# Loading the first weights in halves and the first condition ahead of a threshold, in a conditioned ternary feed-forward kernel

## The chip, the cores and the metric

The kernel runs on one core of one Trainium2 chip. Its time is the device time of one execution in microseconds (us); a version is measured in several runs, and the median is compared. Five engines work side by side: TensorE (PE in the profile; its weight loads are PEld), VectorE (DVE), ScalarE (ACT), GpSimd (POOL) and SyncE (SP), which here issues nearly all transfers. Each takes its own instructions in program order and waits for the others through semaphores.

## The reference

x has 128 sequences of 64 channels and 512 positions. Each sequence picks one of 200 conditioning matrices, and a feed-forward layer with ternary weights follows; its result is quantized to 4 bits and added to x. Cut to what matters:

```python
w = weights[conditions]                       # (128, 64, 64), gathered
c = einsum('bct,bcd->bdt', x, w)              # the condition: (128, 64, 512)

def ternarize(W):                             # threshold 0.05
    delta = 0.05 * max(abs(W))                # over the whole matrix
    mask  = abs(W) > delta
    alpha = sum(abs(W) * mask) / max(sum(mask), 1)
    return alpha * sign(W) * mask

h = gelu(c @ ternarize(W1).T + b1)            # 512 -> 2048
y = h @ ternarize(W2).T + b2                  # 2048 -> 512
scale = max(abs(y)) / 7 + 1e-8                # over the whole of y
out = x + clip(round(y / scale), -7, 7) * scale
```

The threshold `delta` needs the largest magnitude of all of W1, so no ternary weight exists before the last piece of W1 has landed.

## The kernel before, in words

The 128 sequences go through in 16 blocks of 8 (four pairs, `PAIRS = 4`, 512 columns). The hidden layer of 2048 is cut into 16 chunks `hc` of 128. Per block and chunk, PE multiplies the condition by the chunk's W1 (`layer1`), ScalarE applies Gelu, and PE multiplies by the chunk's W2 (`layer2`). A value is carried as a high part (fp32r) and a low part (f16), so each product is made twice, `k = 0` and `k = 1`; for the high part GpSimd widens the ternary weights to fp32r (`widen1`, line 369).

The order of all work is written out by hand: every engine is wrapped in `InOrder` (line 28), which keeps its instructions in program order. Nothing is planned by a scheduler. A semaphore that a transfer uses is used again by the eighth transfer after it, which waits for it.

The change concerns the start, before the first block's chunks flow:

- *Loads* (lines 104 to 131). SyncE issues, in this order: `conditions` (the token numbers, 32 KB) into the tile `first`; the four groups of W1 (`nat1`, 1 MB each; how each is cut into pieces stands in `PIECES`, line 113: groups 0 and 1 whole, group 2 in two, group 3 in three); x of block 0 in two halves of two pairs (`load_x`, line 95); b1; W2; b2.
- *Rows and gathers.* DVE makes row numbers from the token numbers (`rows`, five small instructions), and GpSimd gathers one pair's matrices after the other from HBM (`fetch`, line 166; an indirect transfer of 128 rows of 256 bytes).
- *Group by group* (lines 282 to 295), DVE takes the largest magnitude of each piece (`top_1`), and ScalarE makes the signs (`sign1`) and the magnitudes (`abs1`, in place, so after DVE's reduction of the same piece).
- *Warm-up.* PE runs 46 matmuls with no use for their result (`idle`, line 276), issued ahead of all its other work.
- *`diag`.* GpSimd writes the gathered matrices into the diagonal blocks of `diag`, all four pairs in two instructions (`place_all`, line 183; `place`, line 178, does one pair in two).
- *Threshold* (`thresholds`, line 228). It is a generator: DVE reduces `top_1` to one column and spreads it to 128x128 in `first`, PE transposes that (`tops`), and after the first `yield` DVE takes the maximum and makes `delta` and `minus`.
- *Conditions of block 0.* `mix0(j)` (line 300) is pair j's condition on PE; `hi0(j)` copies its high part on ScalarE, `lo0(j)` makes its low part on DVE.
- *Ternary weights of W1.* `mask1` and `signed1` on DVE make a group's ternary weights, the first group in two halves (`parts1`), of two chunks each.
- *First chunks.* `early(hc)` (line 503) makes chunk hc of block 0 into a PSUM bank; chunk 0 in two halves of 256 columns, each of which needs only two pairs. `count1` counts the mask's ones on PE.

These lines set the order around the change; each name queues on its own engine:

```python
315  find = thresholds("w1", top_1, first[:, 3, :P])
316  next(find)                    # up to PE's transpose
317  delta1, minus1 = next(find)
318  for j in range(PAIRS):
319      mix0(j)
```

and from line 600 on: first half of `mask1(0)` and `signed1(0)`; two gathers of block 1; `widen1` of chunks 0 and 1; two more gathers; the rest of `lo0` and `hi0`; `early(0)`, `early(1)`; the second half of `mask1(0)` and `signed1(0)`; `widen1` of chunks 2 and 3; `count1(0)`; `early(2)`.

Of the kernel before, what the change touches and what calls it, by code (L numbers as in the profile page):

```python
# [15 lines left out]
AF = mybir.ActivationFunctionType  # L16
# [23 lines left out]
def tile_cond_ternary_ffn(  # L40
# [12 lines left out]
    pe, act, dve, pool, sp = (  # L53
        InOrder(tc, e) for e in (nc.tensor, nc.scalar, nc.vector, nc.gpsimd, nc.sync)
    )
    B, C, T = x.shape
# [4 lines left out]
    PAIRS = 4  # L61
    BLK = PAIRS * P
    NB = B // (2 * PAIRS)
    NG = 4
    GH = NH // NG
# [39 lines left out]
    first = big.tile([P, 4, P], F32, tag="big", name="first")  # L105
    cond_i, cond_f, wrap = (first[:, i, : B // 2] for i in range(3))
    cond_i = cond_i.bitcast(I32)
    sp.dma_start(out=cond_i, in_=conditions)


    nat1, nat2 = [], []

    PIECES = [[slice(0, GH)], [slice(0, GH)], [slice(0, 2), slice(2, GH)]]
    PIECES.append([slice(0, 2), slice(2, 3), slice(3, GH)])
    W1f = W1.rearrange("p k c h -> p k (c h)")
    for g in range(NG):
        w = big.tile([P, GH, T], F32, tag="big", name=f"nat1_{g}")
        for ks in PIECES[g]:
            sp.dma_start(out=w[:, ks, :], in_=W1f[:, g * GH :, :][:, ks, :])
# [36 lines left out]
    def half_of(h):  # L156
        return slice(h * C, (h + 1) * C)
# [20 lines left out]
    def place(n, j):  # L178
        for h in range(2):
            out = diag[half_of(h), j, h * D : (h + 1) * D]  # L180
            pool.tensor_scalar(out, gathered[n][half_of(h), j, :], UP, None, ALU.mult)

    def place_all(n):
        for h in range(2):
            out = diag[half_of(h), :, h * D : (h + 1) * D]
            pool.tensor_scalar(out, gathered[n][half_of(h)], UP, None, ALU.mult)
# [3 lines left out]
    def parts(n):  # L190
        return [
            big.tile([P, NT, BLK], t, tag="big", name=f"x{k}_{n}")
            for k, t in enumerate((F32R, F16))
        ]
# [6 lines left out]
    def pair_of(xt, j):  # L201
        return xt[j // 2][:, j % 2, :]

    def mix(xp, j, pc):

        for c in range(NT):
            pe.matmul(
                out=pc[:, c, :],
                lhsT=xp[:, c * P : (c + 1) * P],
                rhs=diag[:, j, :],  # L210
                start=True,
                stop=True,
            )
# [7 lines left out]
    def spread(top1, out, wide_top, space=ps_c, tag="pc"):  # L221

        dve.tensor_copy(wide_top, top1.to_broadcast([P, P]))
        tops = space.tile([P, P], F32, tag=tag, name=f"tops_{out.name}")
        pe.transpose(tops, wide_top, ident_f)
        return tops

    def thresholds(w, top, room):

        top1 = const.tile([P, 1], F32, name=f"top1_{w}")  # L230
        dve.tensor_reduce(top1, top, AX.X, ALU.max)
        delta = const.tile([P, 1], F32, name=f"delta_{w}")
        tops = spread(top1, delta, room)
        yield
        dve.tensor_reduce(delta, tops, AX.X, ALU.max)
        dve.tensor_scalar(delta, delta, THRESHOLD, None, ALU.mult)
        minus = const.tile([P, 1], F32, name=f"minus_{w}")
        dve.tensor_scalar(minus, delta, -1.0, None, ALU.mult)
        yield delta, minus
# [9 lines left out]
    def flat(w):  # L249
        return w.rearrange("p a b -> p (a b)")  # L250


    signs = [big.tile([P, 2, WCH], BF16, tag="big", name=f"signs_{i}") for i in range(2)]
# [3 lines left out]
    above = junk[:, 0, :]  # L257
    top_1 = const.tile([P, sum(map(len, PIECES))], F32)
    sums1 = const.tile([P, NG], F32)

    def group1(tiles, g):
        return tiles[g // 2][:, g % 2, :]

    def sign1(g):
        act.activation(group1(signs, g), flat(nat1[g]), AF.Sign)

    mags = nat1[: NG - 1]

    def abs1(g):

        if g == NG - 1:
            mags.append(big.tile([P, GH, T], F32, tag="big", name="mag"))
        act.activation(flat(mags[g]), flat(nat1[g]), AF.Abs)


    idle = ps_h.tile([P, T], F32, tag="ph", name="idle")
# [6 lines left out]
    for g in range(NG):  # L283
        for ks in PIECES[g]:
            dve.tensor_reduce(
                top_1[:, at : at + 1],
                flat(nat1[g][:, ks, :]),
                AX.X,
                ALU.max,
                apply_absolute_value=True,  # L290
            )
            at += 1
        if g < NG - 1:
            sign1(g)
            abs1(g)
    place_all(0)
    two_next = parts(0)
    pcs = []

    def mix0(j):  # L300
        home, tag = [(ps_c, "pc"), (ps_h, "ph"), (ps_y, "py0"), (ps_y, "py1")][j]
        pc = home.tile([P, NT, P], F32, tag=tag, name=f"pc_0_{j}")
        mix(pair_of(x_next, j), j, pc)
        pcs.append(pc)
# [4 lines left out]
    def lo0(j):  # L309
        part = slice(j * P, (j + 1) * P)  # L310
        dve.tensor_tensor(
            two_next[1][:, :, part], pcs[j], two_next[0][:, :, part], ALU.subtract
        )

    find = thresholds("w1", top_1, first[:, 3, :P])
    next(find)
    delta1, minus1 = next(find)
    for j in range(PAIRS):
        mix0(j)
    hi0(0)  # L320
    hi0(1)
# [1 line left out]
    def mask1(g, part=slice(0, WCH)):  # L323

        dve.tensor_scalar(
            group1(masks, g)[:, part], flat(mags[g])[:, part], delta1, None, ALU.is_gt
        )
# [64 lines left out]
    halves = slice(0, HALF), slice(HALF, BLK)  # L392
# [10 lines left out]
                    stop=(c == NT - 1 and k == 1),  # L403
                )

    def layer1_0(n, hc, ph, part=slice(0, BLK), between={}):
        g, i = divmod(hc, GH)
        narrow = group1(terns, g)[:, i * T : (i + 1) * T].rearrange("p (c h) -> p c h", c=NT)
        for k in range(2):
            w = narrow if k else wide1[n, hc]  # L410
            for c in range(NT):
                between.get((k, c), lambda: None)()
                pe.matmul(
                    out=ph,
                    lhsT=w[:, c, :],
                    rhs=cond[n][k][:, c, part],
                    start=(c == 0 and k == 0),
                    stop=(c == NT - 1 and k == 1),
                )
# [80 lines left out]
    ring = [t[:, i, :] for t in rings for i in range(2)]  # L500
    ring += [quarter.tile([P, BLK], F32, tag="quarter", name=f"ring_{i}") for i in (10, 11)]

    def early(hc, between={}):

        slot = (hc + 4) % 6
        if slot < 2:
            ph = ps_h.tile([P, BLK], F32, tag="ph", name=f"ph_0_{hc}")
        else:
            ph = ps_y.tile([P, BLK], F32, tag=f"py{slot - 2}", name=f"ph_0_{hc}")
        for part in halves if hc == 0 else [slice(0, BLK)]:  # L510
            layer1_0(0, hc, ph[:, part], part, between)
        waiting[hc] = ph

    def early_bend(hc):
        if hc % 2 == 0:
            pairs0[hc // 2] = big.tile([P, 2, 2, BLK], F32R, tag="big", name=f"h_{hc}")
        two = [pairs0[hc // 2][:, hc % 2, k, :] for k in range(2)]
        on_pool = hc in (0, 2, 4, 6)
        bend(0, hc, waiting.pop(hc), two, ring[hc % len(ring)], pool if on_pool else None)
# [91 lines left out]
    hi0(3)  # L611
    lo0(2)
    lo0(3)
    early(0)
    early(1)
    mask1(0, parts1[1])
    signed1(0, parts1[1])
    widen1(0, 2)
    widen1(0, 3)
    abs1(3)  # L620
    for g in range(NG):
        above1(g)
    number = ps_c.tile([P, 1], F32, tag="pc", name="number")
    count1(0)
    early(2)
    mask1(1)
    signed1(1)
# [24 lines left out]
    def behind(hc):  # L652
        if hc == 6:
            largest2(0)
        if 6 <= hc < 6 + NG - 1:
            largest2(hc - 5)
        if hc == 7:
            sign1(3)
        if hc == 8:
            signed1(3)  # L660
        if hc == 11:
            delta.extend(next(find))
            signed2(0)
        if hc == 12:
            for i in (1, 3):
                low(0, i)
            signed2(1)
        if hc in (13, 14):
            widen2(0, hc - 13)
# [19 lines left out]
    for hc in range(NH - LAG):  # L689
# [13 lines left out]
        if hc in (5, 7, 9, 11):  # L703
            j = (hc - 5) // 2
# [189 lines left out]
    order = [*range(AWAY, NB - 2), *range(AWAY), NB - 2]  # L894
# [211 lines left out]
    while s < len(steps):  # L1106
        n, hc = steps[s]
# [10 lines left out]
    n = NB - 1  # L1118
# [108 lines left out]
```

## Time and profile before

| | us |
|---|---|
| median of 3 runs (964.82 to 965.25) | 965.01 |
| the profiled execution's own time | 964.97 |
| its span, first to last instruction | 963.2 |
| PE busy | 951.2 (99%) |
| DVE busy | 708.2 (74%) |
| GpSimd busy | 703.7 (73%) |
| ScalarE busy | 637.1 (66%) |
| granted TensorE clock, mean | 0.999 |

The profile is one execution, and its times count from the start of the span. All compute instructions are recorded through the wrapper's line, L36, so groups are told apart by their tiles: `nat` is a weight matrix as loaded, `top` its largest magnitudes, `wg` the gathered matrices, `pc` a condition in PSUM, `x` its high and low parts, `terns` the ternary weights, `wf` the widened ones, `ph` a chunk in PSUM, `py` the second layer's result. A row of a timeline is start, length, engine, operation, output<-input and shapes, count, and in brackets the idle time before it with what ended it. The chain of waits follows the work that ended last back to the start. Idle time of an engine that nobody waits for costs nothing.

### The profile page before, as it was taken

The page shows a single profiled execution, that of the slowest core. Times are in us where ns is not written, and L with a number is a line of the kernel's source. Part 1 is how long each engine was busy: PE and PEld are TensorE (multiplying, and loading weights), DVE is VectorE, ACT ScalarE, POOL GpSimd, SP SyncE. Part 2 cuts the span into 40 slices and gives each one's busy share as a digit, 9 for nine tenths or more (in the row PEclk, how much of TensorE's full clock was granted, in tenths as well). Part 3 has the DMA queues.
Part 4 walks back from the last instruction along what each step waited for, and adds up shares of the span by engine and source line. Part 5 has one row for each costly group of instructions (what it writes and reads, how often), then busy time and mean ns, then how long its engine had stood idle before and what let it go on. Part 6 is the DMA issues. An engine that isn't in the chain of part 4 may idle for free.

```text
span 963.2 us, 17595 instructions
## 1 busy us (share of the span) xinstructions
PE 951.2 (99%) x6072; PEld 739.9 (77%) x6072; DVE 708.2 (74%) x1239; ACT 637.1 (66%) x1148; POOL 703.7 (73%) x1060
## 2 busy tenths in 40 slices
PE   8999999999999999999999999999999999999997
PEld 4687667888788787787778788788788878778774
DVE  7999766666676766666676676766667798888976
ACT  7995446656656566665656656666665777877774
POOL 5866867677686776767777686776767879788771
PEclk9999999999999999999999999999999999999999
DMA  9301011110111100111020111100131284575741
GB/s 357 103 23 47 14 33 49 33 60 15 35 49 34 60 24 28 55 36 49 25 69 15 34 50 33 59 26 24 49 128 53 65 289 168 191 239 183 274 180 67
DMA packets 33195, 80.11 MB, mean 83 GB/s; under 512 B 3792, under 2 KB 3792, under 8 KB 30160
## 3 DMA queue, kind: packets, MB, share of 16 engines
q1 hardware_dynamic: 31056, 76.86, 23.1%
q0 software_dynamic: 2048, 2.10, 0.7%
q8 instruction: 49, 0.80, 0.3%
q14 instruction: 42, 0.34, 0.1%
HBM read 46.44 MB, written 32.51 MB: 82 GB/s over the span
## 4 chain that ended last, share of the span: by engine, by line
PE 95%; DVE 2%; ACT 1%; DMA 1%; issue 0%; POOL 0%; SPq 0%; ACTq 0%; DVEq 0%
PE py L36 46%; PE xy L36 21%; PE z L36 16%; PE pc L36 6%; PE ph L36 6%; DMA nat<-in_L_ffn_W 1%; DVE top L36 1%; DVE xt L36 0%; ACT ring L36 0%; DVE y_last L36 0%; ACT diag L36 0%; DVE ring L36 0%; POOL wf L36 0%; ACT h L36 0%; PE number L36 0%
## 5 line engine op out<-in xcount | busy, mean ns | idle before, releaser
L36 PE MATMUL py<-wf,h 128*128 128x512 f32 x1088 | 316.2, 416 | 0.0
L36 POOL CAST wf<-w2t 128x512 fp32r<-128x512 fp8e4 x240 | 227.3, 966 | 106.7 <-PE py L36 103.6
L36 POOL CAST wf<-sums 128x256 fp32r<-128x256 fp8e4 (+1 forms) x336 | 181.2, 545 | 88.4 <-PE xy L36 85.0
L36 DVE SCALAR_TENSOR_TENSOR low_parts<-ring,h 128x512 f16<-128x512 f32 x232 | 206.0, 925 | 40.0 <-ACT h L36 40.0
L36 PEld LDWEIGHTS py<-wf,h 128*128 128x128 f32 x1088 | 196.5, 189 | 44.0
L36 ACT ACTIVATE ring<-ring,b1t,alpha_up 128x512 f32<-128x512 f32 x224 | 181.6, 818 | 63.4 <-DVE ring L36 58.6
L36 PE MATMUL py<-w2t,low_parts 128*128 128x512 fp8e4 x920 | 218.7, 379 | 0.0
L36 DVE TENSOR_TENSOR ring<-xy,ring 128x256 f32<-128x256 f32 x224 | 124.1, 554 | 120.3 <-PE xy L36 120.2
L36 ACT COPY ring<-xy 128x256 f32<-128x256 f32 x224 | 83.3, 372 | 174.0 <-PE xy L36 172.7
L36 PEld LDWEIGHTS <-low_parts 128*128 128x128 f16 x920 | 90.1, 98 | 84.1 <-issue 0.3
L36 ACT ACTIVATE h<-ring 128x512 fp32r<-128x512 f32 x240 | 138.6, 626 | 0.7
L36 POOL CAST wf<-w1t 128x256 fp32r<-128x256 fp8e4 (+1 forms) x240 | 132.5, 567 | 2.7 <-PE xy L36 0.3
L36 PE MATMUL xy<-xb,wf 128*128 128x256 f32 x448 | 98.8, 301 | 0.0
L36 PE MATMUL xy<-xt,wf 128*128 128x256 f32 x448 | 88.2, 278 | 1.0 <-ACT ring L36 0.6
L36 PE MATMUL xy<-xl,sums 128*128 128x256 f16 x448 | 87.9, 278 | 0.0
L36 PE MATMUL xy<-xl,w1t 128*128 128x256 f16 x448 | 86.6, 275 | 0.0
L36 PE MATMUL z<-xl,sums 128*128 128x256 f16 x448 | 85.5, 273 | 0.7 <-ACT ring L36 0.6
L36 PEld LDWEIGHTS xy<-xt,wf 128*128 128x128 f32 x448 | 76.2, 188 | 11.6 <-POOL wf L36 1.1
L36 PEld LDWEIGHTS xy<-xb,wf 128*128 128x128 f32 x448 | 75.8, 189 | 10.3
L36 PEld LDWEIGHTS <-sums 128*128 128x128 fp8e4 x896 | 69.2, 97 | 15.9 <-issue 1.2
L36 DVE TENSOR_TENSOR ring<-z,ring 128x256 f32<-128x256 f32 x112 | 47.2, 421 | 41.2 <-PE z L36 40.7
L36 POOL DMA_INDIRECT wg<-in_L_cond_weights,rows x64 | 64.0, 1000 | 18.3 <-issue 8.7
(126 smaller groups left out, 1342.2 us busy)
## 6 DMA issues: line engine op xcount, KB each, us to landing
xt<-in_x SPq DMA_DIRECT2D x36, 512.0 KB
y_dram<-y SPq DMA_DIRECT2D x15, 1024.0 KB
out<-xt SPq DMA_DIRECT2D x30, 512.0 KB
x_quarters<-in_x SPq DMA_DIRECT2D x56, 256.0 KB
nat<-in_L_ffn_W SPq DMA_DIRECT2D x6, 1024.0 KB
y_back<-y_dram SPq DMA_DIRECT2D x2, 1024.0 KB
nat<-in_L_ffn_W SPq DMA_DIRECT2D x3, 512.0 KB
wg<-in_L_cond_weights,rows POOLq DMA_INDIRECT x64, 2.5
```

The costliest lines, as they stand in the source:

```text
L36: return lambda *args, **kw: self._tc.keep_in_program_order(make(*args, **kw))
```

## The change

There are four edits, all at the start:

1. The token numbers are issued from ScalarE's queue; W1 is SyncE's first issue.
2. Group 0 of W1 is loaded in two halves, and its reductions, signs and magnitudes are made by halves.
3. `diag` is written pair by pair, and pair 0's condition stands ahead of the threshold's transpose on PE.
4. Chunks 0 and 1 are both made in halves of 256 columns, in a crosswise order (`early_two`): (chunk, half, k) = 000, 001, 010, 100, 101, 011, 110, 111.

```diff
-    sp.dma_start(out=cond_i, in_=conditions)
+    act.dma_start(out=cond_i, in_=conditions)
...
-    PIECES = [[slice(0, GH)], [slice(0, GH)], [slice(0, 2), slice(2, GH)]]
+    PIECES = [[slice(0, 2), slice(2, GH)], [slice(0, GH)], [slice(0, 2), slice(2, GH)]]
...
-    def sign1(g):
-        act.activation(group1(signs, g), flat(nat1[g]), AF.Sign)
+    def sign1(g, ks=slice(0, GH)):
+        out = group1(signs, g)[:, ks.start * T : ks.stop * T]
+        act.activation(out, flat(nat1[g][:, ks, :]), AF.Sign)
...
-    def abs1(g):
+    def abs1(g, ks=slice(0, GH)):
...
-        act.activation(flat(mags[g]), flat(nat1[g]), AF.Abs)
+        act.activation(flat(mags[g][:, ks, :]), flat(nat1[g][:, ks, :]), AF.Abs)
...
-            sign1(g)
-            abs1(g)
-    place_all(0)
+            pieces = PIECES[g] if g == 0 else [slice(0, GH)]
+            for ks in pieces:
+                sign1(g, ks)
+            for ks in pieces:
+                abs1(g, ks)
+    for j in range(PAIRS):
+        place(0, j)
...
     find = thresholds("w1", top_1, first[:, 3, :P])
+    mix0(0)
     next(find)
     delta1, minus1 = next(find)
-    for j in range(PAIRS):
+    for j in range(1, PAIRS):
         mix0(j)
...
-    def layer1_0(n, hc, ph, part=slice(0, BLK), between={}):
+    def layer1_0(n, hc, ph, part=slice(0, BLK), between={}, ks=range(2)):
...
-        for k in range(2):
+        for k in ks:
...
-    def early(hc, between={}):
+    def bank(hc):
...
-        for part in halves if hc == 0 else [slice(0, BLK)]:
-            layer1_0(0, hc, ph[:, part], part, between)
         waiting[hc] = ph
+        return ph
+
+    def early(hc, between={}):
+
+        layer1_0(0, hc, bank(hc), between=between)
+
+    def early_two():
+
+        phs = [bank(hc) for hc in range(2)]
+        order = [(0, 0, 0), (0, 0, 1), (0, 1, 0), (1, 0, 0), (1, 0, 1), (0, 1, 1)]
+        for hc, h, k in order + [(1, 1, 0), (1, 1, 1)]:
+            layer1_0(0, hc, phs[hc][:, halves[h]], halves[h], ks=(k,))
...
-    early(0)
-    early(1)
+    early_two()
```

## The prediction

> **What bounds the kernel now.** I read the page first: PE is busy 951.2 of 963.2 us, and the chain that ended last is 95% PE, so a change pays only where PE stands still. By stretches of time, PE lacks 3.8 us before 24.56 us (and 12.7 of its 20.8 busy ones there are warm-up matmuls), none from 24.56 to 62, 1.7 up to 950 and 6.5 in the last 13.2. The whole change acts in the first stretch. So I read next the chain of waits from the start, in order of time (start, length, what):
>
> ```profile
> 1.66 7.15 DMA nat<-in_L_ffn_W
> 8.84 6.86 DVE top L36 x6
> 16.20 0.33 PE tops_delta_w L36
> 16.53 3.60 PE pc L36 x32
> 20.14 0.59 ACT x L36
> 20.76 0.69 DVE x L36
> 21.45 0.67 DVE masks L36
> 22.15 0.70 DVE terns L36
> 22.91 1.61 POOL wf L36
> 24.56 3.90 PE ph L36 x16
> ```
>
> Seen here: W1's second group lands at 8.81; six reductions follow without a gap; then the threshold, the four conditions (`pc`), the last high and low part of x (`ACT x`, `DVE x`), the second half of group 0's mask and ternary weights, and GpSimd's widening for chunk 2. PE starts chunk 2 at 24.56 and has no gap for the next 37 us, so the end of the run moves with this moment. Then the timeline of single engines, with the idle time before each row:
>
> ```profile
> 1.19 3.64 SPq L36 DMA_DIRECT2D nat<-in_L_ffn_W  x7
> 2.66 0.29 DVE L36 CAST first<-first 128x64 f32<-128x64 int32 x1 [0.61 <-DMA first<-in_itok_B]
> 6.33 2.29 DVE L36 TENSOR_REDUCE top<-nat 128x1 f32<-128x2048 f32 x1 [2.37 <-DMA nat<-in_L_ffn_W]
> ...
> 4.25 1.17 POOL L36 DMA_INDIRECT wg<-in_L_cond_weights,rows  x1 [1.35 <-DVE rows L36]
> 14.07 1.78 POOL L36 TENSOR_SCALAR diag<-wg 64x256 f32<-64x256 f32 x2 [4.90 <-DMA wg<-in_L_cond_weights,rows]
> 16.12 1.01 POOL L36 DMA_INDIRECT wg<-in_L_cond_weights,rows  x1 [0.27 <-POOL diag L36]
> 17.43 1.29 POOL L36 DMA_INDIRECT wg<-in_L_cond_weights,rows  x1 [0.30 <-issue]
> 18.76 1.17 POOL L36 CAST wf<-terns 128x512 fp32r<-128x512 bf16 x2
> ...
> 20.76 0.69 DVE L36 TENSOR_TENSOR x<-pc,x 128x512 f16<-128x512 f32 x1 [0.20 <-ACT x L36]
> 22.91 6.25 POOL L36 CAST wf<-terns 128x512 fp32r<-128x512 bf16 x4 [0.60 <-DVE terns L36]
> 24.56 1.21 PE L36 MATMUL ph<-x,wf 128*128 128x512 f32 x4 [0.27 <-POOL wf L36]
> ```
>
> Three slacks stand here: DVE waits 0.20 us before the last low part, GpSimd 0.60 before the widening for chunk 2, PE 0.27 before chunk 2. GpSimd is a second chain as long as DVE's: token numbers land (2.66), `rows`, gathers, `diag`, two further gathers, and the first widening at 18.76 starts when the gather ahead of it ends at 18.72. Last, two tiles asked for by themselves: the gathers' time to landing, first in the first 40 us, then from 85 to 400 us, and the shapes that write `diag` (ns, minimum/median/maximum):
>
> ```profile
> DMA to landing us min/median/max: 5.4/5.8/6.4
> ...
> DMA to landing us min/median/max: 2.3/2.5/5.1
> ...
> L36 POOL TENSOR_SCALAR diag<-wg x116: 360/367/1812, 14.1 to 878.9; 64x64 f32<-64x64 f32 x112, 64x256 f32<-64x256 f32 x4
> ```
>
> **The change part by part.** Sums are against the profiled execution: 964.97 us, 963.2 of span and 1.77 around it; the median of the three runs is 965.01, so what is added to the one holds for the other within 0.04.
>
> *W1 first, in halves.* SyncE's first issue becomes W1's, so the stream starts 0.45 us earlier (1.19 against 0.74). Against that, group 0 now goes in two 512 KB pieces. SyncE's later issues, each of which waits for an earlier piece, come 1.43 us apart (10.26, 11.69, 13.12) for pieces of 512 KB, 2.86 per MB; the 1 MB piece of group 1 took 8.84 - 6.33 = 2.5. So halving costs 0 to 0.36, and group 1 lands 0.1 to 0.45 earlier; I take 0.25, the middle, since the gathers share the row with the 1.43. The halves themselves bring DVE nothing: group 0 is reduced before group 1 lands in either form. The six reductions then end at 15.44, and the threshold's input is ready at 15.9 instead of 16.15. ScalarE's Sign and Abs start earlier and end some 1.5 us earlier (18.1 to 16.6), so the first high part no longer waits for them; the later ones wait for PE. The extra reduction, two extra activations and the extra DMA issue lie in idle time of their engines (2.37 us before the first reduction, 4.10 before the first Sign, SyncE idle from 5.4); without that cover each costs under 0.5.
>
> *First condition ahead of the threshold.* PE takes its work in program order. Its warm-up matmuls end near 15.5. `mix0(0)` now comes next and waits for x's first half. That half follows W1's last piece (landed by 14.61, when the issue that waits for it goes out) by 512 KB, so about 1.4 us later, 16.0; the 0.25 makes it 15.75. One condition takes 3.60 / 4 = 0.90, so the threshold's transpose goes out at 16.65, not 16.20: 0.45 later, although its input is ready at 15.9. The bounds: +0.2 (x there before the warm-up ends: 15.5 + 0.9) and +0.7 (x as late as before). Behind it on DVE wait delta, the first mask, the first ternary half, and the four low parts. The last low part had 0.20 of slack; mask, ternary half and widening follow directly. So by DVE chunk 2 starts 0.45 - 0.20 = 0.25 later (0 to 0.5). The conditions end 0.45 earlier (0.90 moved forward, 0.45 lost), but that only feeds ScalarE's copies, which are then not late.
>
> *`place` pair by pair.* Two 64x256 instructions become eight of 64x64. In the build the first needs only the first gather, the other seven all four. Seven of 0.36 are 2.5 us against 1.78: GpSimd is 0.75 later (0.4 if they overlap as the two casts do, 1.17 for 2 x 0.61; 1.3 with the 0.44 from start to start that pairs of them show later). Behind them queue two gathers, the widenings for chunks 0 and 1, two more gathers, and the widening for chunk 2, whose slack is 0.60 plus DVE's 0.25. So this alone is covered; it uses up the cover.
>
> *Token numbers from ScalarE's queue.* This removes 0.45 from SyncE and adds a 0.39 us issue to ScalarE, which idles until W1 lands: nothing. But the 32 KB no longer go alone and first. They start together with the stream, on the same 16 DMA engines. Whatever later time (call it d) they land moves `rows`, the gathers, `diag` and all that GpSimd does up to chunk 2, one for one. The trace has no transfer on ScalarE's queue. Lower bound: 0, DVE takes them at 2.66 as now. Upper bound: a gather moves the same 128 rows of 256 bytes on a queue other than W1's, and needs 5.8 us to land under the stream, 2.5 without: 3.3. Between the two I take 1.0: the stream is only starting, and what competes is W1's first half, which I estimate to land at 6.33 - 0.45 - 1.25 + 0.1, about 4.7; even sharing to its end would be d = 2.0, and 1.0 is the middle of that and of no contention.
>
> The Trainium skill, DMA: Bandwidth & Descriptors, section Issuing engines are not separate DMA queues, says that DMAs from different engines interleave on the same 16 engines and that using several saves only issue time; its section Queues, rings and completion order has each DMA engine take turns packet by packet. By this rule the eight rows per engine would take turns with the eight of W1's half, d would be near 2.0 and the sum +2.2 us; the row of this case taken above gives +1.2.
>
> *Chunks 0 and 1 crosswise.* The 256-wide pieces take 0.56 and 0.37 us from start to start, the 512-wide 1.0 and 0.87, so the work is equal, 3.7 us. It fills PE's waits, but chunk 2 waits for GpSimd: from the first widening's end to chunk 2 PE needs 3.7 + 0.54 for the counts, GpSimd longer. Worth nothing while DVE or GpSimd is later; its cost is 0 to 0.1.
>
> **Sum.** Chunk 2 starts later by 0.25 + max(0, 0.75 + d - 0.85), at d = 1.0: 0.25 + 0.9 = 1.15 us. Behind it PE has next to no gap that could take it back. 964.97 + 1.15 gives 966.1.
>
> **The rivals.**
> - *Cancelled* (d under 0.3): the token numbers land as now, 0.1 to 0.5 us remain: 965.1 to 965.4. For it: ScalarE can issue at the same moment as SyncE. Against it: the gathers' 5.8 against 2.5.
> - *Slower by more than 0.2%* (1.93 us; about what a measurement of this kernel can tell from no change): one mechanism, the token numbers behind W1's halves. It decides from d = 1.8 on; at d = 2.0 the sum is 2.15, 967.1; at the full 3.3 it is 3.45, 968.4 (DVE's reductions would then also wait for `rows`). For it: the gathers' row, the even sharing. Against it: the engines are empty when both start.
> - *Faster*: the earlier stream reaches chunk 2. It needs x before 15.5, the threshold only 0.2 later, and d near 0; then DVE has 0.1 to give, and GpSimd's 0.60 bounds the rest: 964.4 to 964.9, not beyond 0.2%. Against it: `mix0(0)` stands before the threshold on PE in any case.
>
> **How the numbers follow.** Likeliest case (d from 0.3 to 1.8, 965.3 to 966.9): 0.48. Cancelled: 0.15. Slower beyond 0.2%: 0.31. Faster: 0.06, of which 0.03 beyond 0.2% by something that I don't see. So faster 0.03, same 0.66, slower 0.31. The range leaves out half of the faster cases and the top third of the slower: 964.8 to 967.9.
>
> **What will show it.** The first reduction near 4.7; group 1's near 8.6; the first gather's issue at 4.25 + d (this alone decides between the cases); the threshold's transpose at 16.65 right behind `mix0(0)`; the casts for chunk 2 starting near 24.1 with no wait for `terns`; PE's chunk 2 at 25.7, waiting for GpSimd. Wrong it would be if the token numbers land before 3, if PE shows gaps after chunk 2 that it didn't have, or if what lies around the span (1.77) grows with a second queue.

## The result and the profile after

The change makes the kernel slower by half a per cent. The changed kernel takes 970.37 us (median of six runs, 970.16 to 971.95) against 964.96 for the kernel before in the same sitting, 5.4 us more; the ratio on record, which is not the quotient of the two medians, is 1.0059, with a 95% interval from 1.0049 to 1.0069. The forecast of 966.1 and its range up to 967.9 are both missed. The profiled execution of the changed kernel took 970.16, its span is 968.4, so 1.76 lies around the span as before (1.77).

The moment to look at is again the start of chunk 2 on PE, 24.56 us before. This is the beginning of the chain of waits of the kernel after, in order of time (start, length, what):

```profile
0.74 4.34 DMA first<-in_itok_B
...
6.60 1.17 POOL wg L36
...
10.57 5.59 DMA wg<-in_L_cond_weights,rows
...
16.33 0.37 POOL diag L36
...
19.92 1.11 POOL wg L36
...
22.33 1.63 POOL wf L36 x2
...
24.11 1.71 POOL wg L36
...
26.12 0.91 POOL wg L36
...
28.28 0.63 POOL wf L36
...
28.95 3.88 PE ph L36 x16
```

Before, this stretch of the chain ran over W1, DVE's six reductions, PE's conditions and DVE's second mask. None of that is in it now. It is GpSimd's chain from end to end: token numbers, gathers, `diag`, two gathers, the first widenings, two gathers, the widening for chunk 2. (The row of 26.12 breaks off at a semaphore record inside the gather; the timeline has the gather whole, 2.15 us.) The timelines of the single engines in the same kernel give the times (start, length, engine, operation, and in brackets the idle time ahead of the row with what ended it):

```profile
4.92 1.06 ACT L36 ACTIVATE signs<-nat 128x1024 bf16<-128x1024 f32 x1 [2.25 <-DMA nat<-in_L_ffn_W]
...
5.10 0.20 DVE L36 CAST first<-first 128x64 f32<-128x64 int32 x1 [3.05 <-DMA first<-in_itok_B]
...
8.73 6.85 DVE L36 TENSOR_REDUCE top<-nat 128x1 f32<-128x2048 f32 x6 [0.17 <-DMA nat<-in_L_ffn_W]
...
18.06 0.29 DVE L36 TENSOR_REDUCE delta_w<-tops_delta_w 128x1 f32<-128x128 f32 x1 [2.02 <-PE tops_delta_w L36]
...
24.42 1.27 DVE L36 TENSOR_SCALAR masks<-nat,delta_w 128x2048 bf16<-128x2048 f32 x1
...
26.87 1.28 DVE L36 TENSOR_SCALAR masks<-nat,delta_w 128x2048 bf16<-128x2048 f32 x1
28.07 3.67 DVE L36 TENSOR_SCALAR masks<-mag,delta_w 128x2048 bf16<-128x2048 f32 x1
...
16.75 1.16 PE L36 MATMUL pc<-diag,xt 128*128 128x128 f32 x8 [1.42 <-POOL diag L36]
17.75 0.27 PE L36 MATMUL tops_delta_w<-ident_f,first 128*128 128x128 f32 x1
...
28.95 1.19 PE L36 MATMUL ph<-x,wf 128*128 128x512 f32 x4 [1.63 <-POOL wf L36]
...
16.33 3.31 POOL L36 TENSOR_SCALAR diag<-wg 64x64 f32<-64x64 f32 x7 [3.50 <-DMA wg<-in_L_cond_weights,rows]
...
24.11 1.71 POOL L36 DMA_INDIRECT wg<-in_L_cond_weights,rows  x1 [0.15 <-issue]
26.12 2.15 POOL L36 DMA_INDIRECT wg<-in_L_cond_weights,rows  x1 [0.30 <-issue]
28.28 2.27 POOL L36 CAST wf<-terns 128x512 fp32r<-128x512 bf16 x4
```

To be seen here: DVE takes the token numbers at 5.10, not at 2.66, and just 0.18 us after W1's first half became usable (ScalarE's first Sign, 4.92). DVE's reductions, 8.73 to 15.58, are as early as before, so the threshold's data are not the trouble. Yet the threshold's transpose goes out at 17.75 instead of 16.20, because `mix0(0)` stands in front of it and itself waits for `diag`. The widening for chunk 2 starts at 28.28 with no wait: GpSimd is late, and PE waits 1.63 us for it. And the last two gathers take 1.71 and 2.15 us; they took 0.97 and 0.95. These are their rows in the kernel before, and DVE's mask beside the second:

```profile
20.08 0.97 POOL L36 DMA_INDIRECT wg<-in_L_cond_weights,rows  x1
21.36 0.95 POOL L36 DMA_INDIRECT wg<-in_L_cond_weights,rows  x1 [0.30 <-issue]
...
21.37 0.74 DVE L36 TENSOR_SCALAR masks<-nat,delta_w 128x1024 bf16<-128x1024 f32 x1
```

Chunk 2 starts 4.39 us late. Followed along GpSimd, each term as the difference of the same rows in the two kernels:

| step on GpSimd | later by, us |
|---|---|
| first gather's issue, 4.25 to 6.60 | +2.35 |
| its last gather lands, 14.07 to 16.33 | -0.09 |
| `diag` from there on, 1.78 to 3.31 | +1.53 |
| next two gathers, to the first widening | -0.23 |
| first two casts, 1.17 to 1.63 | +0.46 |
| last two gathers, 0.97 and 0.95 to 1.71 and 2.15 | +1.94 |
| wait of 0.60 before the widening, gone | -0.60 |
| start of the widening to PE's start, 1.65 to 0.67 | -0.98 |
| **chunk 2** | **+4.38** |

The remaining 0.8 us (970.16 - 964.97 = 5.19 in the profiled pair) come later: 0.2 up to 90 us, some 0.4 near 610 us, and 0.25 in the last 12 us, where PE's granted clock is 0.80 instead of 0.89. The 0.2 is also seen with W1's halves alone, and the 0.4 goes with `diag` pair by pair (last section); neither is explained. Whether the clock is the cause of the last term was not tried.

### The profile page after: what moved, and what is told of

Same layout as the page of the kernel before. It is cut to its first block, busy times and chain, and to the rows that moved or that the text cites. A ratio compares the mean times of both kernels' runs of the same rounds, so it can differ in the third digit from the quotient of the medians.

```text
span 968.4 us, 17623 instructions
## 1 busy us (share of the span) xinstructions
PE 951.9 (98%) x6080; PEld 740.7 (76%) x6080; DVE 709.3 (73%) x1240; ACT 637.6 (66%) x1150; POOL 706.1 (73%) x1066
## 3 DMA queue, kind: packets, MB, share of 16 engines
q0 software_dynamic: 2048, 2.10, 0.7%
## 4 chain that ended last, share of the span: by engine, by line
PE 93%; DVE 2%; POOL 1%; ACT 1%; issue 1%; DMA 1%; ACTq 0%; DVEq 0%; POOLq 0%
PE py L36 45%; PE xy L36 21%; PE z L36 15%; PE ph L36 6%; PE pc L36 6%; ACT ring L36 1%; POOL wg L36 1%; DMA wg<-in_L_cond_weights,rows 1%; DVE xt L36 0%; DMA first<-in_itok_B 0%; DVE low_parts L36 0%; DVE ring L36 0%; POOL diag L36 0%; DVE y_last L36 0%; ACT h L36 0%
```

## The experiments

My theory once the result was known: nearly all of the loss is the late token numbers; the transfer takes turns with W1's first piece and lands when that piece lands, whatever its size. The rivals: the new order (pairwise `diag`, a condition ahead of the threshold) is what costs, because GpSimd and PE are pushed past their slack; or the halves of W1 are. Each part was therefore done alone or undone alone; then came runs on what was left over. Times are medians; ratios are against the kernel before on the same chip, which took 964.80 to 964.82.

**The token numbers back on SyncE, ahead of W1; all else as changed.**

```diff
-    act.dma_start(out=cond_i, in_=conditions)
+    sp.dma_start(out=cond_i, in_=conditions)
```

> The changed kernel with one edit undone: the token numbers are SyncE's first issue again. Theory (the tokens): their late landing, 5.10 instead of 2.66, is what made the changed kernel slower, by way of the gathers and GpSimd. Then DVE takes them near 2.7, the first gather issues near 4.3, PE starts chunk 2 between 24.8 and 26, and the time is 965.2 to 966.5. Rival (the order): the condition ahead of the threshold and the pairwise writing of diag hold up DVE and GpSimd, and the tokens only fill slack. Then the transpose stays near 17.7, chunk 2 starts after 27.5 and the time is 968.5 or more.

Measured: 965.97 us (965.86 to 966.11), ratio 1.0012, interval 1.0002 to 1.0021. The tokens are taken at 2.53, the first gather goes out at 4.26, chunk 2 starts at 25.04, and the last two gathers take 0.97 and 1.14. In DVE's and PE's timelines:

```profile
2.53 0.43 DVE L36 CAST first<-first 128x64 f32<-128x64 int32 x1 [0.47 <-DMA first<-in_itok_B]
...
25.04 1.21 PE L36 MATMUL ph<-x,wf 128*128 128x512 f32 x4 [0.36 <-POOL wf L36]
```

With this one line undone the excess over the kernel before falls from 5.4 us to 1.2. So the line is most of the loss, and 1.2 us remain for the other parts.

**The kernel before, with the token numbers alone on ScalarE's queue** (W1's first group whole).

```diff
-    sp.dma_start(out=cond_i, in_=conditions)
+    act.dma_start(out=cond_i, in_=conditions)
```

> The kernel before with one edit: the token numbers are issued from ScalarE's queue, W1 whole and first on SyncE's. Theory (the tokens): they share the DMA engines with W1's first group, whose rows are 8 KB here and not 4 KB. If the engines take turns packet by packet, the tokens land with the end of the whole group, 5.9 to 6.5, and the time is 969 to 972, more than with the halves; if the share is by time or bytes, they land near 5.1 and the time is 967.5 to 970. Rival (the order): chunk 2 stays within 0.7 of 24.56 and the time is 965 to 966.

Measured: 971.14 us (970.82 to 971.32), ratio 1.0065, interval 1.0048 to 1.0082. Alone, the line costs 6.3 us, more than the whole change. The tokens are taken at 6.39, 0.18 us after the 1 MB group became usable (ScalarE's first Sign at 6.21). The first gather goes out at 7.88, and all four conditions wait for `diag`. The timelines of ScalarE, DVE and PE in this run have these rows:

```profile
6.21 1.91 ACT L36 ACTIVATE signs<-nat 128x2048 bf16<-128x2048 f32 x1 [3.53 <-DMA nat<-in_L_ffn_W]
...
6.39 0.20 DVE L36 CAST first<-first 128x64 f32<-128x64 int32 x1 [4.34 <-DMA first<-in_itok_B]
...
20.36 5.78 PE L36 MATMUL pc<-diag,xt 128*128 128x128 f32 x32 [2.98 <-POOL diag L36]
```

And two stretches of the same run (length, busy time and instructions of PE, its weight loads, DVE, ACT and POOL, then PE's granted clock, that is the share of TensorE's full clock that it was given, the DMA share and GB/s):

```profile
18.00:20.00 2.00, 0.00 (x0) 0.00 (x0) 1.56 (x3) 1.28 (x1) 1.92 (x2) 0.50 1.04 430
...
26.00:28.00 2.00, 2.00 (x19) 1.78 (x18) 1.80 (x3) 1.82 (x2) 0.43 (x1) 1.00 0.72 253
```

Two things are seen. PE has next to nothing to do from 15.2 us (the end of its warm-up) to 20.4, its granted clock falls to 0.50, and the four conditions take 5.78 us where the same row of the kernel before has 3.74. So some 2 us of this run's loss are not the late data but PE's clock after the wait for it. And the chain is now DVE's again, since conditions, low parts and the second mask all shift; the widening for chunk 2 waits 2.51 us for `terns`.

**Why the tokens land with W1's first piece.** The trace has a record for each packet. Here are the 144 records of the tokens' transfer (128 packets of 256 bytes, and 16 of 4 bytes that come at its end), sixteen at a time in order of time, since there are 16 DMA engines; the record doesn't name the engine. Shown is the start of the first of each sixteen, beside the packets of W1's first piece:

```
first piece        W1's packet, median   tokens: first start of each sixteen (us)                  last ends
256 KB             2048 B, 0.08 us       2.10 2.39 2.56 2.65 2.75 2.80 2.88 2.98 3.07              3.21
512 KB (after)     4096 B, 0.16 us       2.50 2.94 3.27 3.48 3.66 3.81 3.96 4.05 4.27              4.55
1 MB               8192 B, 0.31 us       2.44 3.23 3.58 3.91 4.23 4.55 4.87 5.14 5.33              5.86
```

A token packet itself takes 0.018 us. The next sixteen come about one W1 packet later: 0.32 us apart beside packets of 0.31, some 0.1 apart beside packets of 0.08. The first piece, like the tokens, is 128 packets, eight for each engine if they are spread evenly, so the two end together: a packet of 256 bytes pays for a turn of 4 KB. The Trainium skill, DMA: Bandwidth & Descriptors, section Queues, rings and completion order, has each DMA engine take turns between its queues packet by packet, and so far the rows agree. But it puts some 9 to 17 descriptors into a packet; the eight token rows of an engine would then pass in a single turn. In these records the turn is one row, and the measurement decides.

**W1's first half in two quarters, otherwise as changed** (first piece 256 KB).

```diff
-    PIECES = [[slice(0, 2), slice(2, GH)], [slice(0, GH)], [slice(0, 2), slice(2, GH)]]
+    PIECES = [[slice(0, 1), slice(1, 2), slice(2, GH)], [slice(0, GH)], [slice(0, 2), slice(2, GH)]]
```

> The changed kernel with W1's first half cut in two quarters, of 2 KB a row. Theory (the engines take turns between the two queues packet by packet, so the tokens' eight rows per engine land with the eighth W1 packet per engine): the tokens land with the first quarter, 3.9 to 4.4 instead of 5.10; the first gather issues at 5.4 to 5.9; the time falls by 0.5 to 1.5 to 968.8 to 969.9. Rival (the second queue has a fixed delay of its own, or the share is by time): the tokens land at 4.9 to 5.3 and the time stays at 970.1 to 970.7.

Measured: 967.02 us (966.90 to 968.61), ratio 1.0028, interval 1.0016 to 1.0040; chunk 2 at 26.44. The first rows of DVE and ScalarE that wait for a transfer in this run:

```profile
3.59 1.32 ACT L36 ACTIVATE signs<-nat 128x512 bf16<-128x512 f32 x2 [0.92 <-DMA nat<-in_L_ffn_W]
...
3.76 0.20 DVE L36 CAST first<-first 128x64 f32<-128x64 int32 x1 [1.72 <-DMA first<-in_itok_B]
...
7.75 1.22 DVE L36 TENSOR_REDUCE top<-nat 128x1 f32<-128x1024 f32 x1 [1.60 <-DMA nat<-in_L_ffn_W]
10.38 6.85 DVE L36 TENSOR_REDUCE top<-nat 128x1 f32<-128x2048 f32 x6 [1.41 <-DMA nat<-in_L_ffn_W]
```

Again the tokens come 0.17 us after the first piece. This settles it: 3.59 and 3.76 for 256 KB, 4.92 and 5.10 for 512 KB, 6.21 and 6.39 for 1 MB. The smaller piece takes the excess from 5.4 us to 2.2. Tokens and time both lie below what was expected: the tokens come 1.34 us earlier than in the changed kernel, but chunk 2 comes 2.51 earlier, because the last two gathers are hardly stretched here (0.97 and 1.15). The smaller piece also has a price, seen in the one traced execution, that I did not foresee: the second half of the group lands only at 7.75 and group 1 at 10.38 (8.73 in the kernel after), since W1's stream moves 190 to 290 GB/s between 4 and 7 us where the changed kernel's moves 430 to 450. Ten of the 8 KB packets that start between 4.5 and 5.5 us take 0.8 to 2.2 us each, where 0.31 is usual; why is not shown.

**The kernel before, with `diag` pair by pair alone.**

```diff
-    place_all(0)
+    for j in range(PAIRS):
+        place(0, j)
```

> The kernel before with one edit: diag of block 0 written pair by pair. Theory (GpSimd's chain sets chunk 2 in the kernel with the first condition ahead, too): GpSimd ends diag near 17.2 instead of 15.85, no longer waits for the ternary half before chunk 2, chunk 2 starts at 25.0 to 25.3 and the time is 965.4 to 966.0, like the run with the condition ahead as well. Rival (DVE behind the later threshold sets it): chunk 2 starts before 24.75 and the time is 964.7 to 965.1.

Measured: 965.68 us (965.56 to 966.00), ratio 1.0009, interval 0.9999 to 1.0019. GpSimd's and PE's timelines:

```profile
14.08 3.05 POOL L36 TENSOR_SCALAR diag<-wg 64x64 f32<-64x64 f32 x7 [3.00 <-DMA wg<-in_L_cond_weights,rows]
...
24.93 1.17 PE L36 MATMUL ph<-x,wf 128*128 128x512 f32 x4
```

The last seven instructions take 3.05 us (14.08 to 17.13) where the two of before took 1.78. The first widening starts at 20.10 instead of 18.76, PE waits 0.63 for it before chunk 0, and chunk 2 starts at 24.93, 0.37 late, without a wait for GpSimd: PE itself is behind. The slack did not cover the edit. The other half of the 0.9 us comes much later, in the step near 610 us (last section).

**The same with the first condition ahead of the threshold too.**

```diff
+    mix0(0)
     next(find)
     delta1, minus1 = next(find)
-    for j in range(PAIRS):
+    for j in range(1, PAIRS):
         mix0(j)
```

> The kernel before with one edit: diag written pair by pair, and the first condition ahead of the threshold's transpose; tokens, W1 whole, chunks 0 and 1 as before. Theory (the tokens): without late tokens this costs little: the transpose goes out at 16.9 (x's first half lands at 15.95, one condition takes 0.9), GpSimd ends diag near 17.2 instead of 15.85, chunk 2 starts at 25.2 to 26.0, and the time is 965.6 to 966.5. Rival (the order): chunk 2 starts after 27.5 and the time is 968 or more.

Measured: 965.98 us (965.71 to 966.57), ratio 1.0012, interval 1.0002 to 1.0022; chunk 2 at 25.21. The place on PE's timeline:

```profile
16.19 1.13 PE L36 MATMUL pc<-diag,xt 128*128 128x128 f32 x8 [1.03 <-DMA xt<-in_x]
17.15 0.27 PE L36 MATMUL tops_delta_w<-ident_f,first 128*128 128x128 f32 x1
```

With the tokens in time, `mix0(0)` waits for x (16.19), and the transpose goes out 0.95 us later than before. The two order edits together cost 1.2 us, which is what was left in the first experiment; 0.65 of it is at chunk 2, and the step near 610 us is in this trace too.

**W1's first group in halves alone; chunks 0 and 1 crosswise alone; both together.** The edits are those of the change: `PIECES` with `sign1` and `abs1` by pieces, and `early_two` in place of `early(0)`, `early(1)`.

```diff
-    PIECES = [[slice(0, GH)], [slice(0, GH)], [slice(0, 2), slice(2, GH)]]
+    PIECES = [[slice(0, 2), slice(2, GH)], [slice(0, GH)], [slice(0, 2), slice(2, GH)]]
...
-    early(0)
-    early(1)
+    early_two()
```

> The kernel before with one edit: W1's first group loaded, reduced, signed and made absolute in halves; tokens still first on SyncE's queue. Both theories: group 1 lands 0 to 0.4 later than 8.81, the first reduction starts at 5.2 to 5.6, and chunk 2 starts at 24.56 to 25.0: 965.0 to 965.5. If halving alone cost more than 1 us, both would have missed a cause.

> The kernel before with one edit: chunks 0 and 1 crosswise in halves. Both theories: PE ends chunk 1 and the counts up to 0.3 us earlier and waits as long for GpSimd, chunk 2 stays at 24.4 to 24.7 and the time at 964.6 to 965.1.

> The kernel before with the two parts that cost nothing by themselves: W1's first group in halves (behind the token numbers on SyncE) and chunks 0 and 1 crosswise. Theory A (both lie beside the two chains that set chunk 2): 964.8 to 965.1, chunk 2 at 24.3 to 24.6. Theory B (together they gain, because the crosswise order fills the wait that earlier signs leave on PE): 964.4 to 964.7.

Measured: halves 965.01 us (964.89 to 965.06), ratio 1.0001, interval 0.9991 to 1.0011; crosswise 964.86 (964.69 to 965.07), 1.0001, 0.9991 to 1.0010; both 965.03 (964.82 to 965.61, eleven runs), 1.0002, 0.9993 to 1.0011. Chunk 2 starts at 24.46, 24.30 and 24.60, the first two a tenth of a us ahead of the expected stretch. Neither part does anything that can be measured, and neither do the two together; so no version found here beats the kernel before.

**What stretched the last two gathers: the changed kernel, with them behind the widenings of chunks 2 and 3.**

```diff
-    for j in range(2, PAIRS):
-        fetch(1, j)
...
     widen1(0, 2)
     widen1(0, 3)
+    for j in range(2, PAIRS):
+        fetch(1, j)
```

> The changed kernel with one thing moved: the last two gathers of block 1 stand on GpSimd behind the widenings for chunks 2 and 3, not ahead of them. Theory (the tokens push these gathers under DVE's masks, where they took 1.71 and 2.15 us instead of 0.97 and 0.95): the widening for chunk 2 starts near 24.6, and chunk 2 is bound by PE itself, which ends the counts near 27.3; chunk 2 starts at 27.2 to 27.5 instead of 28.95, and the time is 968.4 to 969.0. Rival (the gathers' length is a matter of the record only, and something else holds the widening): chunk 2 stays at 28.5 or later and the time is above 969.8.

Measured: 969.23 us (969.10 to 969.32), ratio 1.0045, interval 1.0028 to 1.0062: 1.14 us less than the changed kernel, though 0.2 above the theory's range. In GpSimd's, PE's and DVE's timelines of this run:

```profile
24.82 3.16 POOL L36 CAST wf<-terns 128x512 fp32r<-128x512 bf16 x2 [0.60 <-DVE terns L36]
28.14 2.24 POOL L36 DMA_INDIRECT wg<-in_L_cond_weights,rows  x1 [0.16 <-issue]
30.68 1.53 POOL L36 DMA_INDIRECT wg<-in_L_cond_weights,rows  x1 [0.30 <-issue]
...
27.45 1.17 PE L36 MATMUL ph<-x,wf 128*128 128x512 f32 x4
...
32.89 1.18 PE L36 MATMUL ph<-x,wf 128*128 128x512 f32 x4 [0.41 <-POOL wf L36]
...
28.98 1.27 DVE L36 TENSOR_SCALAR masks<-mag,delta_w 128x2048 bf16<-128x2048 f32 x1
```

Chunk 2 starts at 27.45, 1.50 earlier than in the changed kernel, and no longer waits for GpSimd; 0.41 of that goes again into a wait before chunk 4 (32.89). The gathers are just as stretched in their new place, because masks of DVE run there too. A gather that meets a 2048-wide mask ends right after it: the first here at 28.14 + 2.24 = 30.38, the mask at 28.98 + 1.27 = 30.25. In the changed kernel the two gathers end at 25.82 and 28.27, DVE's masks at 25.69 and 28.15. It is so again with `diag` pair by pair alone (24.20 after 24.07) and in the control below (28.29 after 28.17). Five times 0.12 or 0.13 us: that reads as a wait for DVE, not as a slower gather. It is not so for every mask. In the kernel before, the gather of 21.36 starts with the 1024-wide mask of 21.37 and takes 0.95 all the same. The Trainium skill, SBUF — State Buffer, section Who interferes with whom, gives the mechanism: GpSimd has no read and write port of its own but shares one pair with DVE, under an exclusive lock. The stretched rows fit that; no run here shows the lock itself, or at which moment of its issue a gather needs the ports. One row does not fit so simply: the second gather here takes 1.53 us and ends 0.82 after DVE's last instruction of that time.

**The same move in the kernel before, as a control.** The edit is the one above.

> The kernel before, with the last two gathers of block 1 behind the widenings of chunks 2 and 3. A control for the same move in the changed kernel, where it gave 1.14 us. Theory A (that gain came from gathers lying under DVE's masks and so taking 1.71 and 2.15; here they take 0.97 and 0.95 ahead of them): GpSimd is ready for chunk 2 some 2 us earlier but waits for DVE's terns, chunk 2 starts at 24.4 to 24.6, and the time is 964.8 to 965.2, up to 0.4 more if the gathers, now under the masks of the next groups, delay chunk 4. Theory B (the move itself is a gain, wherever the gathers lie): 963.9 to 964.4.

Measured: 968.11 us (966.21 to 969.41, ten runs), ratio 1.0028, interval 1.0019 to 1.0037. Both theories missed. The start of chunk 2, at 24.40, is as theory A had it; the loss comes after it. GpSimd's and PE's timelines:

```profile
26.05 2.24 POOL L36 DMA_INDIRECT wg<-in_L_cond_weights,rows  x1 [0.15 <-issue]
28.59 1.54 POOL L36 DMA_INDIRECT wg<-in_L_cond_weights,rows  x1 [0.30 <-issue]
...
30.81 2.07 PE L36 MATMUL ph<-x,wf 128*128 128x512 f32 x4 [1.35 <-POOL wf L36]
```

And stretches of the same execution (columns as above, the granted clock behind POOL):

```profile
31.00:33.00 2.00, 2.00 (x7) 1.61 (x8) 0.00 (x0) 0.00 (x0) 1.53 (x3) 0.50 0.02 4
35.00:37.00 2.00, 2.00 (x6) 1.03 (x5) 2.00 (x1) 1.97 (x3) 0.79 (x2) 0.50 0.00 0
```

The gathers, now under masks, take 2.24 and 1.54 in front of the widening for chunk 4, and PE waits 1.35 us for it. In the profiled execution, the longest of the ten at 969.41, the clock is then 0.50 until some 37 us, and four matmuls take 2.07 instead of 1.18. The ten times fall into groups: 966.2 (three, mean clock 0.998), 968.0 to 968.4 (six, 0.996 or 0.997) and 969.41 (0.995). The first group is the plain wait, 964.81 + 1.35 = 966.16; that the others owe their 2 to 3 us to the clock is seen in the profiled one, and for the six it follows only from their mean clock. For the question asked: the move is no gain of itself, so in the changed kernel it gained by taking stretched gathers off the path to chunk 2.

**The tokens on ScalarE's queue with W1's halves and the crosswise order, but `diag` and the threshold in the old order.**

```diff
-    for j in range(PAIRS):
-        place(0, j)
+    place_all(0)
...
-    mix0(0)
     next(find)
     delta1, minus1 = next(find)
-    for j in range(1, PAIRS):
+    for j in range(PAIRS):
         mix0(j)
```

> The changed kernel with the order at the threshold taken back (diag in two instructions, no condition ahead of the threshold); the token numbers stay on ScalarE's queue beside W1's half. Theory A (the loss is a late GpSimd chain, and the stretched gathers are an accident of how GpSimd's and DVE's work then overlap): tokens taken near 5.1, diag from 16.3 to some 18.4, all four conditions wait for it, so DVE's masks move with the gathers as they did in the run with the tokens alone, the last two gathers take 0.97 and 0.95, and chunk 2 starts 2.0 to 2.5 late, at 26.6 to 27.1: 967.0 to 967.6. Theory B (the tokens' cost is a fixed 4.4 us, as between the changed kernel and the one with the tokens first on SyncE, whatever the order): chunk 2 at 28 to 29, 969.0 to 969.5, and the gathers over 1.5 each.

Measured: four runs, 967.73, 967.83, 969.34 and 970.76 (mean clocks 0.998, 0.998, 0.996, 0.995), median 968.59, ratio 1.0046, interval 1.0031 to 1.0061. The median lies between two kinds of run; the profiled one is that of 967.83, with the clock at 1.00 through the whole start. From its timelines:

```profile
22.49 0.97 POOL L36 DMA_INDIRECT wg<-in_L_cond_weights,rows  x1 [0.15 <-issue]
23.77 0.95 POOL L36 DMA_INDIRECT wg<-in_L_cond_weights,rows  x1 [0.30 <-issue]
25.29 6.25 POOL L36 CAST wf<-terns 128x512 fp32r<-128x512 bf16 x4 [0.56 <-DVE terns L36]
...
18.65 3.84 PE L36 MATMUL pc<-diag,xt 128*128 128x128 f32 x32 [2.22 <-POOL diag L36]
...
26.94 1.21 PE L36 MATMUL ph<-x,wf 128*128 128x512 f32 x4 [0.37 <-POOL wf L36]
```

Chunk 2 starts at 26.94, in the 26.6 to 27.1 of theory A, and the gathers take 0.97 and 0.95; all four times lie above its 967.0 to 967.6, the lowest by 0.1. All conditions wait for `diag` here, so DVE's masks move together with GpSimd's gathers: the 2048-wide ones start at 25.14, after the last gather's end at 24.72. (That gather does lie beside the 1024-wide mask of 23.75, as in the kernel before, without being stretched.) In the changed kernel the first condition and the threshold go ahead, DVE's 2048-wide masks come early in comparison (24.42), GpSimd comes late (`diag` takes 1.2 us longer), and they meet. So the parts don't add up: late tokens with the old order cost 2.38 us at chunk 2, the new order with timely tokens 0.48 to 0.65 (25.04 and 25.21), the two together 4.39.

## Why the prediction was wrong

*What bounds the kernel.* Right. The end moves with the start of chunk 2, and the chain that passed to GpSimd was named. From chunk 2 to 62 us PE has no gap in either kernel; of 5.19 us in the profiled pair, 4.39 are there.

*W1 first and in halves.* The mechanism was right, and small as said: group 1 lands 0.11 us earlier (8.84 to 8.73), in the range of 0.1 to 0.45 though not the 0.25 taken. The threshold's input is ready at 16.04, not at 15.9. The first reduction was forecast near 4.7 and comes at 6.22, although the half is there at 4.92: DVE takes `first` and `rows` in program order ahead of it, and they wait for the tokens. That costs nothing, since group 1 is the later one.

*First condition ahead of the threshold.* Failed, in the step that took x's arrival as what `mix0(0)` waits for, with the transpose at 16.65. It goes out at 17.75, 1.55 later than before instead of 0.45. With late tokens, `mix0(0)` waits for its `diag`: this needs two instructions, the second of which stands behind all four gathers, at 16.33. The prediction noted that the other seven wait for all four, and did not carry it over to PE. With tokens in time x does decide, but it comes at 16.19 and not at 15.75, and the transpose is 0.95 late, beyond the bound of 0.7 as well. That bound was wrong by its own working: before, the conditions did not wait for x at 16.53, so x could be as late as that, and 16.53 + 0.90 would have been 1.23 late.

*`place` pair by pair.* The term was mis-sized: 0.75 taken, up to 1.3 allowed; measured 1.27 alone and 1.53 in the changed kernel. The instructions come 0.43 us apart, as the bound of 0.44 from the pairs later in the trace had it, and the 0.36 taken leaves out the gap between them. In the change the last takes 0.72 beside DVE's first mask. "This alone is covered" is wrong too: alone it delays chunk 2 by 0.37, because the first widening comes after PE is ready for chunk 0, a wait that the slack before chunk 2 does not measure; the time grows by 0.9 (interval -0.1 to 1.8), with the step near 610 us.

*Token numbers from ScalarE's queue.* The term that was mis-sized by most: d was taken as 1.0, the middle of no contention and even sharing; it is 2.44 at DVE (2.66 to 5.10) and 2.35 at the gathers. Even sharing to the end of W1's half, 2.0 by the estimate, was the answer; and the half ends at 4.9, not at 4.7, so it is a little more. There was no reason for the middle: the argument that the engines are empty when both start speaks about the first turn alone, and there are eight. The estimate by turns packet by packet, which the prediction set beside its row, was the better one of the two, though its sum, 2.2 us, was still short. It took one row for a packet, which is not what the page that it names says, as set out above, but what the records of this case show.

*Crosswise.* Right: nothing.

*The sum.* Its form holds as far as it goes. With the measured d and `diag` it gives 0.25 + max(0, 1.53 + 2.35 - 0.85) = 3.28. What lacks to 4.39 is a term that the prediction did not have: GpSimd's gathers and casts under DVE's masks, +0.46 and +1.94, less the 0.98 that the widening for chunk 2 is shorter, and the 0.09 and 0.23 by which the gathers took less. So of the 3.24 us by which chunk 2 was forecast too early (1.15 against 4.39), 1.35 are d, 0.78 are `diag` and 1.42 this term, less those 0.32. The other 0.8 us come behind chunk 2, where the prediction had next to nothing. The run that moves the gathers away shows it with 1.14 us of time. The trace of before held the hint: a gather there took 1.29 beside a ternary half of DVE, others 0.95.

*The rivals.* "Slower" named the mechanism, the token numbers behind W1's halves, and the point from which it decides, d = 1.8; both are right. Its prices, 967.1 at d = 2.0 and 968.4 at 3.3, are too low, for want of that term. "Cancelled" and "faster" are refuted by the first gather's issue at 6.60.

## What to carry to other kernels

A small transfer that others wait for should go ahead of a large one, on the same queue if need be: beside it on a second queue it ended here when the large one's first piece ended, at three sizes of that piece, both being cut into 128 packets. What the issue on the shared queue costs (0.45 us here) can be set against that by looking at the large transfer's first landing in the trace. And when two engines share something, a delay of one is not just carried on: ask which long instructions of the other it will now lie under, for at that point parts that cost 3.0 us (in the executions at the full clock) and 1.2 us alone became 5.4.

## What the runs showed of the hardware that was not expected

- *The granted clock falls after a wait, and costs more than the wait.* In the run with the tokens alone PE had next to nothing to do from 15.2 us on, the clock was 0.50 by 18 us, and the four conditions took 5.78 instead of 3.74; after a wait of 1.35 (and 48 short matmuls of one column ahead of it) it was 0.50 from 31 to 37 us in the control run. The changed kernel itself has waits of 1.42, 2.13 and 1.63 us in its start and a clock of 1.00 there all the time. What makes the difference is not settled by these runs; that one kernel has executions with and without it is what the groups of times in two of the runs suggest. The Trainium skill, TensorE: Matmul & The Clock Gate, section Part 1: The HAM clock gate, has an activity window that runs freely against the kernel, which would make it chance; the two levels, 0.50 and 1.00, agree with it.
- *GpSimd's gather issue waits for a 2048-wide mask of DVE.* 0.95 us free, 1.71, 2.15 and 2.24 where it met one, with its end 0.12 to 0.13 us after the mask's; but 0.95 beside a 1024-wide mask that starts with it. It goes both ways: DVE's mask of 28.07 in the changed kernel took 3.67 us beside GpSimd's casts, where 1.28 is the time without.
- *Smaller pieces of W1 at the start thinned its stream.* With the first half in quarters, group 1 landed 1.65 us later than in the changed kernel, in the one execution that was traced. Open.
- *A step of some 0.4 us near 610 us* goes with `diag` pair by pair. It is in the traces of the changed kernel, of the run with the tokens back on SyncE and of others with the new order, and with that edit alone: there ScalarE's instructions are 0.48 us later than before ahead of it and 0.90 behind it. It is in none of the six runs with `diag` in two instructions. It comes at a time when the queue that loads instructions is active. The run with quarters has `diag` pair by pair too, and not the step. Open.
